# Four graph layers on one core: rows with exchanged batches, loads spread over the first stage, and the last group's third weight recorded into the second stage

## The chip, the cores and the metric

The kernel runs on one core of one Trainium2 chip. Its time is the device time of one execution in microseconds, and the time of a version is the median of its runs. One more execution was recorded by the hardware profiler; every row of a profile below comes from such an execution.

## The reference

`x` has 128 batches of 64 nodes and 256 features, `adj` is 64 x 64, and everything is float32. Four layers follow one another, each as a residual with a layer norm behind it. Cut to what matters:

```python
mix = lambda M, y: einsum('nm,bmh->bnh', M, y)
ln = lambda y: (y - mean(y)) / sqrt(var(y) + 1e-5)        # over the features

# layer 0: three graph steps 256 -> 512 -> 1024 -> 256
S = adj * adj
h = relu(mix(S, x @ W1)); h = relu(mix(S, h @ W2))
x = ln(x + mix(S, h @ W3))

# layer 1: spectral step with the eigenvectors U of adj's normalized Laplacian
h = relu(mix(U.T, x) @ W1 + b1)                            # 256 -> 128
x = ln(x + mix(U, h @ W2 + b2))                            # 128 -> 256

# layer 2: two graph steps, then an LSTM over windows of 1, 2, 3 and 4 nodes
h = relu(mix(adj, x @ Wg0 + bg0)); h = relu(mix(adj, h @ Wg1 + bg1))
for p in 1, 2, 3, 4:       # the last hidden state of each window replaces its last node
    h[last node of each window of p] = lstm_p(windows of h)
x = ln(x + h)

# layer 3: h = x @ W + b_lin; a = softmax over m of (h h^T * adj, zeros masked)
x = ln(x + a @ h + b)
```

## The kernel before

The 8192 rows form 64 row tiles of 128 rows, two batches to a tile, and four tiles (eight batches) form a group: 16 groups. A mixing step multiplies from the left by a 128x128 matrix that holds the 64x64 matrix twice on its diagonal (`adT2`, `sqT2` with the squares, `u2` and `ut2` for the eigenvectors).

**First stage** (`layer0`, called at L1228; groups in the order 4 to 15, then 0 to 3). The rows of the last four groups stay in SBUF (`X`, `RING = 4`). Those of the other twelve lie in `XA` until the stage is done, and each group's result goes to DRAM (`rest`), from where the second stage fetches it. The instruction order of PE, DVE, ACT and POOL is the order of the program text here (`manual_schedule`). For each group:

- `burst` (L1062) mixes and transposes a half of the rows at once: 32 products of 64x64 blocks (two instructions each in float32), four of them on different quarters of PE's array. Its tensors are `ps`, `sqT`, `X` or `h` in the trace.
- `seven` runs a 2x2 block product with seven instead of eight block products, for the first, second and third weight (`by_first`, `by_second`, `by_third`; L977 is the helper `mm` that all of them call). The additions that this needs are on DVE (`VL`, recorded at L52) and as adding DMAs (`adds`). A `step()` puts the copies or additions of one product behind the next one and emits one small step of a pending layer norm.
- the last group uses `plain` (L1121) for the third weight: four products of 8 x two 128x256 instructions, with no additions.
- `mix_rows` (L1136) mixes the result `s3` with `sqT2`: two float32 products of 128x512 in a group, one for each pair of row tiles. Their result is added to the rows, normed, and stored to `rest`.

The eigenvectors come from a Jacobi-like solver (`eigen`) whose steps are inserted between the products by a running clock (`now`, `between`); `u2` and `ut2` are ready at the end of the stage.

All loads are issued by SP ahead of the loop, in the order of the text: `adj`, the first group's rows, the first two weights, then the rows of all other groups with the third weight (`aw3`) after the second group (L921 to L924), then the constants of the solver and the weights and biases of the later layers (L943 to L959). Some small preparations stand behind the first stage in the text (L1235 to L1244: row sums of `adj`, biases added or halved); no manual order covers them, and a scheduler places their instructions.

**Second stage** (`Plan`). Layers 1 to 3 are recorded as operations with costs, and a list scheduler orders them on each engine before anything is emitted; all of them are emitted at L162. Work comes in units of two groups (`unit`), up to four in flight (`UNITS = 4`). Tiles of an operation come from counted slots, and an operation starts when its inputs and slots are there by the planned clock. The first recorded unit, `left_over`, holds the layer norm steps that the first stage has not yet emitted, and the later units depend on them by rows. The weights of the LSTMs (`wih`, `whh`, L1258 to L1267) get the same seven-product treatment, with their sums prepared in `add_weights` (L1305). The last unit (groups 14 and 15, `ENDING`) runs a different end: `from_lstm` (L1526) copies the hidden states `hT` from node-major to batch-major (`hb`), turns them on PE, adds and norms them; `layer3` (L1549) works in two halves and its last norm uses ACT for the scaling. `norm` (L1426) takes the statistics on DVE, and its `rs` (and, in that scalar form, `nm`) on POOL.

Of the kernel before, what the change touches and what calls it, by code (L numbers as in the profile page):

```python
# [16 lines left out]
N = 64  # L17
# [744 lines left out]
P = 128  # L762
# [15 lines left out]
RING = 4  # L778
QUADS = 1.17
# [61 lines left out]
def kernel(  # L841
# [28 lines left out]
    x_t = x.rearrange("b n f -> (b n) f").rearrange("(t p) f -> p t f", p=P)  # L870
    out_t = out.rearrange("b n f -> (b n) f").rearrange("(t p) f -> p t f", p=P)
# [32 lines left out]
    def given(g):  # L904
        return x_t[:, 4 * g:4 * g + 4, :]

    adst = keep.tile([P, N], F32, name="adst")
# [3 lines left out]
    nc.scalar.dma_start(rows_of(order[0])[:, 2:4, :], given(order[0])[:, 2:4, :])  # L911
    for t in range(2):
        nc.sync.dma_start(rows_of(order[0])[:, t, :], given(order[0])[:, t, :])
# [5 lines left out]
    for g in order[1:]:  # L919
        for t in (0, 2):  # L920
            nc.sync.dma_start(rows_of(g)[:, t:t + 2, :], given(g)[:, t:t + 2, :])  # L921
        if g == order[1]:
            aw3 = load(wa, "aw3", a_w3, "(k p) f -> p k f", [P, 8, D], p=P)
    nc.sync.dma_start(eig_c, consts)  # L924
# [11 lines left out]
    sqT2 = ea.tile([P, P], F32, name="sqT2")  # L936
# [14 lines left out]
    nc.sync.dma_start(cb1, c_b1)  # L951
    wide = {}
    for name, src in (("b_b1", b_b1), ("b_b2", b_b2), ("c_b0", c_b0), ("d_b", d_b)):
        wide[name] = keep.tile([P, src.shape[0]], F32, name=f"wide_{name}")
        nc.sync.dma_start(wide[name], src.partition_broadcast(P))
    cbi = keep.tile([P, 4, 8], F32, name="cbi")
    cbh = keep.tile([P, 4, 8], F32, name="cbh")
    nc.sync.dma_start(cbi, c_bi)
    nc.sync.dma_start(cbh, c_bh)  # L959
# [48 lines left out]
    h2 = pa.tile([P, 2, 8, 256], F32, name="h2")  # L1008
    sh = pa.tile([P, 4, 4, 256], F32, name="sh")
    s3 = pa.tile([P, 4, D], F32, name="s3")  # L1010
# [51 lines left out]
    def burst(dst, src, c):  # L1062
        to = dst.rearrange("p c (t h n) -> p h c t n", h=2, n=N)
        p = [bank().rearrange("p (c t n) -> p c t n", c=2, t=4) for _ in range(2)]
        for t in range(4):
            for k in range(2):
                for m, f, h, hs in quads(c + k):
                    PE.matmul(p[h][m, k, t, :], src[hs, t, f], sqT2[hs, hs], start=True, stop=True)  # L1068
        now[0] += QUADS
        between()  # L1070

        def result():
            for h in range(2):
                S.copy(to[:, h, c:c + 2], p[h])

        step(result)
# [44 lines left out]
    def plain():  # L1121
        for t in (0, 2):
            p = bank().rearrange("p (t f) -> p t f", t=2)
            for i in range(2):
                run(p[:, i, :], [(h2[:, t // 2, c, i * P:(i + 1) * P], aw3[:, c, :]) for c in range(8)])
                step((lambda p=p, t=t: S.copy(s3[:, t:t + 2, :], p)) if i else None)
                yield
        for _ in range(3):
            yield

# [5 lines left out]
    def mix_rows(g, t):  # L1136
        p = bank().rearrange("p (t f) -> p t f", t=2)
        mm(p, sqT2, s3[:, t:t + 2, :])

        def result():  # L1140
            x2 = rows_of(order[g])[:, t:t + 2, :]
            VL.tensor_add(x2, p, x2)
            norms.extend(scalar_norm(tc, small, x2, half, spare))
            if t and order[g] >= RING:
                norms.append(lambda: nc.sync.dma_start(rest[order[g]], rows_of(order[g])))

        step(result)

    def sums_second():
        S1, S2, S4 = (ss[:, i] for i in range(3))  # L1150
        VL.tensor_add(S1, A21, A22)
        VL.tensor_sub(S2, S1, A11)
        VL.tensor_sub(A21, A11, A21)
        VL.tensor_sub(S4, A12, S2)

    def layer0():
# [12 lines left out]
        for g in range(n):  # L1169
            last = g == n - 1  # L1170
            then = {} if last else {
                (1, 1): lambda: less(2, 0, 0),
                (1, 6): lambda: sums_first() if g else burst(m1, rows_of(order[1]), 0),
                (0, 5): lambda: (less(2, 1, 0), nc.sync.dma_start(sh[:, 1], sh[:, 2])),
                (0, 3): lambda: (nc.sync.dma_start(sh[:, 0], H22), adds(sh[:, 1], H22)),
                (0, 4): lambda: (less(3, 0, 1), None if g else sums_first()),
                (1, 3): lambda: [adds(sh[:, slot], H21) for slot in range(3)],
            }
            sums_second()
            w2 = [seven(256, by_second(j), *[h2[:, r, 4 * c + 2 * j:4 * c + 2 * j + 2, :] for r in (0, 1) for c in (0, 1)],  # L1180
                        relu, order=(1, 2, 6, 5, 7, 4, 3) if j else (1, 2, 6, 5, 7, 3, 4)) for j in range(2)]
            sums = [] if g else [signed_sums(), sums_of_weights(first[0], W12)]
            for j in (0, 0, 1, 0, 1, 0, 1, 0, 1, 1, 0, 0, 1, 1):
                then.get((j, next(w2[j])), lambda: None)()
                for some in sums[j:]:
                    next(some, None)
            if last:
                for t in (0, 2):
                    mix_rows(g - 1, t)
                for _ in plain():  # L1190
                    pass
                for t in (0, 2):
                    mix_rows(g, t)
                break
            w3 = seven(P, by_third, *[s3[:, r:r + 2, c:c + P] for r in (0, 2) for c in (0, P)], S.copy,
                       order=(1, 2, 5, 6, 7, 3, 4))
            w1 = seven(256, by_first, *[h1[:, r:r + 2, c:c + 256] for r in (0, 2) for c in (0, 256)], relu)
            next(w3)
            less(3, 1, 1)
            if g:  # L1200
                mix_rows(g - 1, 0)
            next(w1)
            next(w3)
            next(w1)
            VL.tensor_sub(X12, X12, sx[:, 1])
            if g:
                mix_rows(g - 1, 2)
            next(w1)
            next(w1)
            adds(sh[:, 3], sh[:, 1])  # L1210
            for w in (w3, w1, w3, w1, w1, w3):
                next(w)
            burst(m2, h1, 2)
            next(w3)
            burst(m2, h1, 0)
            next(w3)
            if g + 2 < n:
                burst(m1, rows_of(order[g + 2]), 0)
# [3 lines left out]
    with tc.manual_schedule(engines={mybir.EngineType.PE, mybir.EngineType.DVE, mybir.EngineType.Activation,  # L1222
                                     mybir.EngineType.Pool}):
# [11 lines left out]
    pr = bank()  # L1235
    PE.matmul(pr[:, :P], ones, adT2, start=True, stop=True)
    V.tensor_copy(rs_row, pr[:, :P])
    V.tensor_scalar(adH2, adT2, 0.5, None, op0=ALU.mult)
    V.tensor_reduce(rs_col, adst, AX.X, ALU.add)
    V.tensor_scalar(wide["c_b0"], wide["c_b0"], rs_col, None, op0=ALU.mult)  # L1240
    V.tensor_add(cbi, cbi, cbh)
    V.tensor_add(dbb, dbb, dbl)
    for q in (slice(0, 4), slice(6, 8)):
        V.tensor_scalar(cbi[:, :, q], cbi[:, :, q], 0.5, None, op0=ALU.mult)  # L1244
# [12 lines left out]
    psb = ctx.enter_context(tc.tile_pool(name="psb", bufs=1, space=bass.MemoryType.PSUM, reuse_waits="tile"))  # L1257
    wih, whh = [], []  # L1258
    for i in range(4):
        if i:  # L1260
# [6 lines left out]
        whh.append(load(wb, f"whh{i}", c_hh[i], "(k p) f -> p k f", [P, 2, 1024], p=P) if i else None)  # L1267
# [37 lines left out]
    def add_weights(p, ready):  # L1305
        ways[p] = []
        names = "igo" if p == 1 else "ifgo"
        for k, w in enumerate((wih[p - 1], whh[p - 1])):
# [6 lines left out]
            s, w = plan.tile("sums", [P, 3, nq, P], s), plan.tile("sums", [P, 2, nq * 2 * P], w)  # L1315
            a11, a12, a21, a22 = whole = quarters(w)
# [109 lines left out]
    def norm(x, scalar, eps=EPS, twice=False):  # L1426
# [4 lines left out]
        if twice:  # L1431
# [4 lines left out]
        if scalar:  # L1436
            nm = plan.tile("nm", [P, 2])
            G.tensor_scalar(nm, mv[:, :, 0], -1.0, None, op0=ALU.mult)
            G.tensor_tensor(nm, nm, rs, ALU.mult)
# [86 lines left out]
    def from_lstm(xs, hT, g):  # L1526
        if g in ENDING:
            hb = as3(work(), 2)
            for bs in (slice(0, 4), slice(4, 8)):
                for k, copy, cost in ((0, V.tensor_copy, 0.33), (1, S.copy, 0.56)):  # L1530
                    copy(as3(hb[:, k, :], 8)[:, bs, :], hT[:, k, :, bs].rearrange("p n b -> p b n"), cost=cost)
# [17 lines left out]
    def layer3(xs, g, first, nt):  # L1549
# [89 lines left out]
        for t in range(0, nt, 2):  # L1639
# [8 lines left out]
            at = 4 * g + first + t  # L1648
            for j in range(2):
                Q.dma_start(out_t[:, at + j, :], x2[:, j, :])  # L1650
# [113 lines left out]
    def long(hTs, p):  # L1764
# [6 lines left out]
        def write(h, o, t):  # L1771
            for w in range(2):
                turn_out(seen(h, w, p - 1), o[:, w], t[:, w])

        c, hs = state("c", 8 * nw), None
        for t in range(p):
            x = [[seen(k, w, t) for w in range(2)] for k in range(2)]
            new = state("hs", 8 * nw) if t < p - 1 else None
            fast(p, 8 * nw, x, hs, c, new, write)
            if p == 4 and t == 2:  # L1780
                plan.late = plan.ops[-1]
            hs = new

    def unit(groups):
# [8 lines left out]
        for g in groups:  # L1793
            plan.group = g + 1
            x = plan.tile("rows", [P, 4, D])
            there.append(plan.tile("rest", [P, 4, D], rest[g]))
            if g < RING:
                x.tile.real, x.tile.slot, x.tile.unit = rows_of(g), g, plan.unit
                plan.slots["rows"][g] = 1e9
                for i, op in enumerate(reversed(plan.pieces)):  # L1800
                    if g == RING - 1 - i // 14:
                        half = np.arange(4 * D) // (2 * D) == i // 7 % 2
# [6 lines left out]
        for p in (3, 4):  # L1809
            long(hTs, p)  # L1810
# [12 lines left out]
    def left_over():  # L1823
# [6 lines left out]
        plan.pieces = plan.ops  # L1830
# [47 lines left out]
```

## Time and profile before

| | before |
|---|---|
| device time, median of 3 runs | 2268.37 us (2267.16 to 2269.09) |
| profiled execution | 2269.74 us, span 2267.9 us |
| mean granted TensorE clock | 0.995 |
| DMA packets, moved | 95243, 163.05 MB |

The span is the time from the first to the last recorded instruction; the 1.84 us beside it lie around the recorded part. Times in the rows are microseconds from the start of the span. PE is the matrix engine, PEld its weight load, DVE the vector engine, ACT the scalar engine, POOL GpSimd, and SP the queue that issues most DMAs. A timeline row has the start, the time from first start to last end, engine, line, operation, output and inputs, the shape, and the number of instructions; in brackets stands the idle time ahead of it and what ended that. A float32 product appears as two matmul instructions.

The page's costliest groups are `ps<-w,wih` (572.8 us of PE in 2944 instructions) and `ps<-w,sums` (476.6 us in 3104), both of the LSTMs, and the chain of work that ended last runs through `ps` at L162 for 59% and `ch` at L977 for 15% of the span. The first stage lasts to about 820 us, some 49 us for a group, and the second from there to the end.

### The profile page before, as it was taken

The page shows a single profiled execution, that of the slowest core. Times are in us where ns is not written, and L with a number is a line of the kernel's source. Part 1 is how long each engine was busy: PE and PEld are TensorE (multiplying, and loading weights), DVE is VectorE, ACT ScalarE, POOL GpSimd, SP SyncE. Part 2 cuts the span into 40 slices and gives each one's busy share as a digit, 9 for nine tenths or more (in the row PEclk, how much of TensorE's full clock was granted, in tenths as well). Part 3 has the DMA queues.
Part 4 walks back from the last instruction along what each step waited for, and adds up shares of the span by engine and source line. Part 5 has one row for each costly group of instructions (what it writes and reads, how often), then busy time and mean ns, then how long its engine had stood idle before and what let it go on. Part 6 is the DMA issues. An engine that isn't in the chain of part 4 may idle for free.

```text
span 2267.9 us, 53164 instructions
## 1 busy us (share of the span) xinstructions
PE 2222.0 (98%) x20840; PEld 2026.8 (89%) x20840; DVE 1758.5 (78%) x5925; ACT 1241.2 (55%) x2999; POOL 207.9 (9%) x390
## 2 busy tenths in 40 slices
PE   7999999999999999999999999999999999999996
PEld 5998888888888878999999999999999999999985
DVE  5888888878888759765967977977977877578977
ACT  3455555545554445665655655655655655566554
POOL 0111111111111110000100000000000010000112
PEclk9999999999999999999999999999999999999998
DMA  8443333344332240000211211211211211002331
GB/s 264 96 92 77 85 75 85 87 91 94 85 85 66 66 155 29 20 1 20 76 38 41 78 66 50 78 57 50 87 57 41 84 65 35 31 29 65 109 113 54
DMA packets 95243, 163.05 MB, mean 72 GB/s; under 512 B 24976, under 2 KB 65936, under 8 KB 94992
## 3 DMA queue, kind: packets, MB, share of 16 engines
q1 hardware_dynamic: 83840, 120.05, 15.8%
q0 software_dynamic: 10800, 39.33, 9.2%
q8 instruction: 164, 2.69, 0.5%
q14 instruction: 87, 0.71, 0.1%
q10 hardware_dynamic: 352, 0.28, 0.0%
HBM read 57.64 MB, written 45.09 MB: 45 GB/s over the span
## 4 chain that ended last, share of the span: by engine, by line
PE 89%; DVE 6%; DMA 2%; ACT 1%; issue 1%; SPq 1%; POOL 1%; ACTq 0%; POOLq 0%; DVEq 0%
PE ps L162 59%; PE ch L977 15%; PE b L977 7%; PE ps L977 6%; PE ps L1068 2%; DVE w L162 1%; PE pa L312 1%; DVE D L52 1%; DMA XA<-in_x_dram 1%; DVE gates L162 1%; DVE X L162 1%; ACT gates L162 0%; DVE h L52 0%; DVE tw L52 0%; SPq L921 0%
## 5 line engine op out<-in xcount | busy, mean ns | idle before, releaser
L162 PE MATMUL ps<-w,wih 128*128 128x128 f32 (+2 forms) x2944 | 572.8, 298 | 2.1 <-DVE gates L162 0.9
L162 PEld LDWEIGHTS ps<-w,wih 128*128 128x128 f32 x2944 | 453.8, 191 | 28.5 <-issue 6.2
L162 PE MATMUL ps<-w,sums 128*128 128x128 f32 (+2 forms) x3104 | 476.6, 293 | 0.0
L162 PEld LDWEIGHTS ps<-w,sums 128*128 128x128 f32 x3104 | 423.5, 191 | 14.1 <-issue 1.9
L162 ACT ACTIVATE gates<-gates,cbi 128x256 f32<-128x256 f32 (+4 forms) x736 | 314.0, 479 | 174.0 <-DVE gates L162 172.0
L162 DVE TENSOR_TENSOR gates<-gates,ps 128x512 f32<-128x512 f32 (+4 forms) x408 | 234.2, 585 | 173.1 <-PE ps L162 159.7
L162 ACT COPY gates<-ps 128x512 f32<-128x512 f32 (+4 forms) x408 | 203.8, 505 | 253.8 <-PE ps L162 247.8
L986 ACT ACTIVATE h<-h 128x512 f32<-128x512 f32 x141 | 88.8, 629 | 283.3 <-DVE h L52 283.2
L162 PE MATMUL ps<-hs,whh 128*128 128x128 f32 (+1 forms) x896 | 181.2, 284 | 0.1
L162 PE MATMUL ps<-w,whh 128*128 128x128 f32 (+1 forms) x896 | 181.1, 284 | 0.0
L162 POOL TENSOR_SCALAR rs<-mv 128x2 f32<-128x2 f32 x96 | 27.5, 297 | 1318.5 <-DVE mv L162 1317.0
L162 ACT ACTIVATE gates<-ps,cbi 128x128 f32<-128x128 f32 (+2 forms) x368 | 119.1, 383 | 43.4 <-PE ps L162 43.1
L162 PEld LDWEIGHTS ps<-hs,whh 128*128 128x128 f32 x896 | 139.7, 191 | 0.3 <-DVE hs L162 0.3
L162 PEld LDWEIGHTS ps<-w,whh 128*128 128x128 f32 x896 | 139.7, 191 | 0.0
L977 PE MATMUL ch<-m,tw 128*128 128x256 f32 x512 | 120.6, 380 | 3.5 <-DVE h L52 3.5
L977 PE MATMUL b<-ss,aw 128*128 128x256 f32 x512 | 122.6, 379 | 0.0
L977 PEld LDWEIGHTS ch<-m,tw 128*128 128x128 f32 x512 | 96.2, 190 | 17.2 <-DVE h L52 4.7
L977 PEld LDWEIGHTS b<-ss,aw 128*128 128x128 f32 x512 | 96.3, 190 | 12.7
L1060 POOL DMA_DIRECT2D sh<-h x60 | 53.2, 957 | 485.9 <-PE b L977 148.8
L162 ACT ACTIVATE gates<-c 128x256 f32<-128x256 f32 (+1 forms) x176 | 75.5, 433 | 27.9 <-DVE c L162 26.2
L162 PE MATMUL ps<-hs,sums 128*128 128x128 f32 (+1 forms) x448 | 90.6, 284 | 0.0
L162 DVE TENSOR_TENSOR w<-w,w 128x128 f32<-128x128 f32 (+2 forms) x264 | 80.5, 316 | 8.9 <-PE ps L162 4.4
(384 smaller groups left out, 4281.2 us busy)
## 6 DMA issues: line engine op xcount, KB each, us to landing
sh<-h POOLq DMA_DIRECT2D x60, 512.0 KB, 5.8
far<-w SPq DMA_DIRECT2D x42, 512.0 KB, 2.8
w<-far SPq DMA_DIRECT2D x168, 128.0 KB, 3.1
X<-rest SPq DMA_DIRECT2D x24, 512.0 KB, 3.4
out_dram<-X SPq DMA_DIRECT2D x64, 128.0 KB, 1.8
sh<-sh SPq DMA_DIRECT2D x15, 512.0 KB, 2.9
sh<-h SPq DMA_DIRECT2D x15, 512.0 KB, 2.9
sh<-sh POOLq DMA_DIRECT2D x15, 512.0 KB, 4.6
```

Of the source, the lines that this page charges most:

```text
L52: return getattr(self.engine, name)(out, *args, **kw)
L162: getattr(e, name)(*[real(x) for x in args], **{k: real(v) for k, v in kw.items()})
L312: PE.matmul(out, lhsT, rhs, start=True, stop=True)
L977: PE.matmul(out, lhsT, rhs, start=start, stop=stop, **kw)
L986: S.activation(dst, src, AF.Relu)
L1060: nc.gpsimd.dma_start(out, src, accum_op=ALU.add)
L1068: PE.matmul(p[h][m, k, t, :], src[hs, t, f], sqT2[hs, hs], start=True, stop=True)
```

## The change

- **Rows with exchanged batches.** Before, half `h` of row tile `t` in a group holds batch `2t + h` of that group. After, tile `2u + j` holds batch `2h + j` of four in half `h` (`given`, `found`). `fetch` therefore loads two tiles by two DMAs of 64 partitions, and the output is stored the same way.
- **Row mixing in quarters.** `mix_rows` takes a whole group at once: eight products of 64x256 on quarters of the array, into two banks, in place of two of 128x512. The result is added and normed by halves `h` (tiles `h` and `h + 2`).
- **Loads spread.** Only the first four groups' rows (`AHEAD = 4`) are loaded ahead; group `g + 4` is fetched at the top of group `g`, with two of the loads in the list `later` (constants, weights, biases) beside it. SP is put into the first stage's manual order.
- **Small preparations** (`small_things`) run inside the first stage, at the end of the products with the second weight of group `n - 4`.
- **Third weight of the last group.** `plain` and its mix leave `layer0` and are recorded in `left_over`, so that the list scheduler places them. `aw3`, `h2`, `s3` and `sqT2` now live through both stages; `aw3` and `h2` share the tile `twice`, into which three LSTM weights (`c_ih[3]`, `c_hh[2]`, `c_hh[3]`) are loaded once those products are over (`plan.over`).
- **Norm.** In the scalar form, `rs` (the addition of epsilon) and `nm` (one instruction in place of two) are on DVE in place of POOL.
- **Ending.** The copies of `hT` to batch-major are made before the last LSTM step of `p = 4`, and that step writes its states there (`turned`).

```diff
+    given, found = (v.rearrange("(q h j) n f -> q h n j f", h=2, j=2) for v in (x, out))
+    def fetch(queue, g, u):
+        for h, hs in enumerate(halves):
+            queue.dma_start(rows_of(g)[hs, 2 * u:2 * u + 2, :], given[2 * g + u, h])
+    twice = keep.tile([P, 3, 8, D], F32, name="twice")
+    aw3, h2 = twice[:, 0], twice[:, 1:3]
...
-    for g in order[1:]:
-        for t in (0, 2):
-            nc.sync.dma_start(rows_of(g)[:, t:t + 2, :], given(g)[:, t:t + 2, :])
+    for g in order[1:AHEAD]:
+        for u in range(2):
+            fetch(nc.sync, g, u)
...
-    nc.sync.dma_start(eig_c, consts)
+    later = [(eig_c, consts)]
...
-    def plain():
-        for t in (0, 2):
-            p = bank().rearrange("p (t f) -> p t f", t=2)
-            for i in range(2):
-                run(p[:, i, :], [(h2[:, t // 2, c, i * P:(i + 1) * P], aw3[:, c, :]) for c in range(8)])
-                step((lambda p=p, t=t: S.copy(s3[:, t:t + 2, :], p)) if i else None)
...
-    def mix_rows(g, t):
-        p = bank().rearrange("p (t f) -> p t f", t=2)
-        mm(p, sqT2, s3[:, t:t + 2, :])
+    def mix_rows(g):
+        p = [bank().rearrange("p (u f) -> p u f", u=2) for _ in range(2)]
+        for u in range(2):
+            for j, js in enumerate(halves):
+                for h, hs in enumerate(halves):
+                    PE.matmul(p[h][js, u, :], sqT2[hs, hs], s3[hs, 2 * u + j, :], start=True, stop=True)
 
         def result():
-            x2 = rows_of(order[g])[:, t:t + 2, :]
-            VL.tensor_add(x2, p, x2)
-            norms.extend(scalar_norm(tc, small, x2, half, spare))
-            if t and order[g] >= RING:
-                norms.append(lambda: nc.sync.dma_start(rest[order[g]], rows_of(order[g])))
+            rows = rows_of(order[g])
+            for h in range(2):
+                VL.tensor_add(rows[:, h::2, :], p[h], rows[:, h::2, :])
+                norms.extend(scalar_norm(tc, small, rows[:, h::2, :], half, spare))
+            if order[g] >= RING:
+                norms.append(lambda: nc.sync.dma_start(rest[order[g]], rows))
...
+    def small_things():
...
         for g in range(n):
+            if g + AHEAD < n:
+                for u in range(2):
+                    fetch(nc.sync, order[g + AHEAD], u)
+            for to, of in later[2 * g:2 * g + 2]:
+                nc.sync.dma_start(to, of)
...
+            if g == n - 4:
+                small_things()
             if last:
-                for t in (0, 2):
-                    mix_rows(g - 1, t)
-                for _ in plain():
-                    pass
-                for t in (0, 2):
-                    mix_rows(g, t)
+                mix_rows(g - 1)
                 break
...
             if g:
-                mix_rows(g - 1, 0)
+                mix_rows(g - 1)
...
-            if g:
-                mix_rows(g - 1, 2)
...
+    wih[3], whh[2], whh[3] = late = [twice[:, i].rearrange("p (k a) f -> p k (a f)", k=2) for i in range(3)]
...
+            if any(w.tile.real is x for x in late):
+                Q.dma_start(w, (c_hh if k else c_ih)[p - 1].rearrange("(k p) f -> p k f", p=P), cost=0.35, after=plan.over)
...
-        if twice:
+        if scalar:
+            V.tensor_scalar(rs, mv[:, :, 1], eps, None, op0=ALU.add)
+        elif twice:
...
-            G.tensor_scalar(nm, mv[:, :, 0], -1.0, None, op0=ALU.mult)
-            G.tensor_tensor(nm, nm, rs, ALU.mult)
+            V.scalar_tensor_tensor(nm, mv[:, :, 0], -1.0, rs, op0=ALU.mult, op1=ALU.mult)
...
     def from_lstm(xs, hT, g):
         if g in ENDING:
-            hb = as3(work(), 2)
-            for bs in (slice(0, 4), slice(4, 8)):
-                for k, copy, cost in ((0, V.tensor_copy, 0.33), (1, S.copy, 0.56)):
-                    copy(as3(hb[:, k, :], 8)[:, bs, :], hT[:, k, :, bs].rearrange("p n b -> p b n"), cost=cost)
+            hb = hT.rearrange("p k b n -> p k (b n)")
...
+            if ending and new is None:
+                for hT in hTs:
+                    turned.append(work().rearrange("p (k b n) -> p k b n", k=2, b=8))
+                    for k, copy in ((0, V.tensor_copy), (1, S.copy)):
+                        copy(turned[-1][:, k], hT[:, k].rearrange("p n b -> p b n"), cost=0.8 if k else 0.6)
             fast(p, 8 * nw, x, hs, c, new, write)
...
     def left_over():
...
+        s, x = plan.tile("s3", [P, 4, D], s3), plan.tile("rows", [P, 4, D], rows_of(order[-1]))
+        for t in (0, 2):
+            p = ps4((P, 2, D))
+            for i in range(2):
+                for c in range(0, 8, 2):
+                    plan.note("PE", [("matmul", (p[:, i, :], h2[:, t // 2, k, i * P:(i + 1) * P], aw3[:, k, :]),
+                                      {"start": k == 0, "stop": k == 7}) for k in (c, c + 1)], 0.87,
+                              after=plan.ops[-1] if i + c else None)
+            plan.over = plan.ops[-1]
+            S.copy(s[:, t:t + 2, :], p)
+        q = [ps4((P, 2, D)) for _ in range(2)]
+        plan.note("PE", [("matmul", (q[h][js, u, :], sqT2[hs, hs], s[hs, 2 * u + j, :]), {"start": True, "stop": True})
+                         for u in range(2) for j, js in enumerate(halves) for h, hs in enumerate(halves)], QUADS)
+        for h in range(2):
+            V.tensor_add(x[:, h::2, :], q[h], x[:, h::2, :])
+            norm(x[:, h::2, :], True)
+        plan.last = x
```

## The prediction

> **What bounds the kernel now.** I read the page's busy shares and its chain first, then PE's waits, a table of stretches, and PE's and DVE's timelines where PE is not full.
>
> ```profile
> PE 2222.0 (98%) x20840; PEld 2026.8 (89%) x20840; DVE 1758.5 (78%) x5925; ACT 1241.2 (55%) x2999; POOL 207.9 (9%) x390
> PE 89%; DVE 6%; DMA 2%; ACT 1%; issue 1%; SPq 1%; POOL 1%; ACTq 0%; POOLq 0%; DVEq 0%
> ```
>
> PE is the bound: a microsecond of product taken away counts wherever PE is full, and idle PE is in three places. The first is the start, where DVE stands behind two loads and PE behind DVE:
>
> ```profile
> 44.48 0.16 DVE L1242 TENSOR_TENSOR dbb<-dbb,dbl 128x2 f32<-128x2 f32 x1 [5.17 <-DMA dbb<-in_d_b_dram]
> 48.24 0.35 DVE L1240 TENSOR_SCALAR wide_c_b<-wide_c_b,rs_col 128x256 f32<-128x256 f32 x1 [2.70 <-DMA wide_c_b<-in_c_b_dram]
> ...
> 45.69 0.46 PE L312 MATMUL pa<-AQ,LV 128*128 128x128 f32 x2 [2.07 <-DVE LV L52]
> 49.24 1.99 PE L977 MATMUL ch<-m,tw 128*128 128x256 f32 x8 [0.51 <-DVE h L52]
> 53.68 1.99 PE L977 MATMUL ch<-m,tw 128*128 128x256 f32 x8 [2.44 <-DVE h L52]
> ```
>
> The second is the seam of the stages: 17.65 us of PE alone (804.02 to 821.67) while DVE has little, then some 60 us in which DVE is full and PE is not. Columns: stretch, its length, busy PE, PEld, DVE, ACT, POOL, granted clock, DMA share, GB/s.
>
> ```profile
> 800.00:825.00 25.00, 24.50 (x226) 19.95 (x225) 4.96 (x9) 8.63 (x24) 2.00 (x5) 1.00 0.39 133
> 825.00:850.00 25.00, 21.24 (x473) 18.44 (x475) 22.55 (x59) 14.05 (x40) 7.78 (x17) 0.93 0.55 214
> 850.00:875.00 25.00, 22.01 (x229) 18.34 (x219) 23.60 (x54) 14.47 (x28) 1.77 (x4) 0.99 0.08 25
> ...
> 805.74 13.98 PE L977 MATMUL ps<-aw,h 128*128 128x256 f32 x64
> 837.63 3.43 PE L162 MATMUL ps<-bw,v 128*128 128x256 f32 x8 [2.70 <-DVE v L162]
> ```
>
> The third is the end, a chain of small steps after the last LSTM product (2224 to 2265). Between, from 60 to 804 and from 885 to 2170, PE idles under 4 us.
>
> **The change, part by part.** *Start.* The additions at L1239 to L1244 leave the head of DVE's queue and run in group `n - 4` of the first stage (`small_things`), and their loads no longer stand behind twelve groups of rows. The PE waits 2.07 + 0.51 + 2.44 = 5.0 us go. What is late next: the second `h<-h,ch` sum follows 3.3 us of eigen steps that need the product now at 43.6, so it ends near 47.6, and PE wants it at 48.1: nothing new. A stall of 1.60 us at 27.05 that the profile puts down to issue, while the DMA share is 1.1, may go too: 0 to 1.6, I take 0. Start: -5.0.
>
> The loads are the same bytes as 64-partition copies, twice as many issues: 0.43 us each, four in each of twelve groups and two small ones in the first eight, at most 2.6 us of SP ahead of the `sh` copies. SP issues nothing between 600.64 and 628.82 in a steady group and the rows are four groups (some 195 us) early: nothing. Without that cover it would be up to 2.6 us for each of twelve groups.
>
> *Row mixing.* Two 128x512 products become eight of 64x256 on quarters of the array. The rows that bear on it:
>
> ```profile
> 607.68 1.02 PE L977 MATMUL ps<-s,sqT 128*128 128x512 f32 x2
> 608.54 1.03 PE L977 MATMUL ch<-aw,m 128*128 128x256 f32 x4
> ...
> 627.10 2.05 PE L977 MATMUL ch<-tv,h 128*128 128x128 f32 x16
> 629.08 1.16 PE L1068 MATMUL ps<-sqT,X 64*64 64x64 f32 x64
> 630.17 1.99 PE L977 MATMUL ch<-m,aw 128*128 128x256 f32 x8
> 632.00 1.89 PE L977 MATMUL ps<-m,aw 128*128 128x256 f32 x8
> ```
>
> From start to start, a 128x512 mix takes 0.86 us, two 1.72. A 256-column instruction takes 1.73 / 8 = 0.216 us. The burst passes 64 instructions of 64 columns in 1.09 us, 17 ns each where one after the other would need 54 ns: better than three run at once. So 16 instructions of 256 columns need 16 x 0.216 / 4 = 0.86 us at best, 1.09 at the burst's overlap of 3.2. Around a burst there is a toll: the sixteen products ahead take 1.98 us (627.10 to 629.08) against 1.79 elsewhere, the eight behind 1.83 against 1.73: 0.29 in all. 0.93 + 0.29 = 1.22 us, nearer the streaming end since long instructions hide issue; 0.50 saved in each of 15 groups: -7.5. Ends: -12.9 (no toll, four at once) and +4.5 (only two at once: 1.73 + 0.29 is 0.30 more, 15 times). The Trainium skill, TensorEngine Tiling, Tiling Modes, says that a change of tiling mode drains the array while tiles of one mode run in parallel. That speaks against more switches; the 0.29 us agrees, and without such a drain the sum would have 12.9 here instead of 7.5.
>
> The mix now takes two banks of three at once and its sums stand together on DVE, which is 88% busy there (43.9 of 50 us): the next product on that ring is over 2 us later, the sums take 1.3. Nothing; up to 0.5 us a group if not.
>
> *Seam.* The 64 instructions of the third weight (13.9 us) and the last mix are recorded in the second stage's plan; the order built from the changed kernel puts 26 of their 32 products among the products ahead of the first `hs,whh`, and six and the mix behind it. Before, that first `hs,whh` stands at 884.60, 62.9 us after 821.67. By the rows' times PE's products in it are 49.1 us, so 13.8 us is idle (8.2 in the waits listed), slow clock or switching. After, they are 57.8 us and DVE's work falls from 53.7 to 51.1 us, since group 3's come later. With both engines nearly full I take 63.5 us for the stretch (62 to 68). Saved: 17.65, less 1.22 for the mix that stays, 2.6 + 1.2 for what is left to do after it, 2.6 for group 3's products passed on, 0.6 longer stretch: -9.4, from -11 to -5. The weights that share SBUF with `h2` and `aw3` come after the last of these products, about 100 us ahead of their first use. What is late next: the eigenvectors. `u2` stood 34 us ahead of its first use (787.7 to 821.67); now nine products and a mix cover it, 5.1 us. It fits, barely.
>
> Part of it is clock: the products at 837.63, behind 2.70 us of idle PE, took 3.43 us where eight take 1.73, at a granted clock of 0.72 from 835 to 840. That 1.7 us is within the 13.8. The Trainium skill, TensorE: Matmul & The Clock Gate, Part 1, has the clock halved only after an idle window of about 3.4 us; by that this loss would stay outside the change, and the sum 1.7 us smaller. The trace has it after 2.70 us, and decides.
>
> *End.* The copies of `hT` (2226.84 to 2228.1 on the path) go ahead of the last cell: -1.2. `nm` leaves POOL, two steps of about 0.2 us and a hand-over, for one on DVE, at three places of the path: -0.4 each, -1.2. The addition of `eps` moves from POOL to DVE too, one hand-over later: -0.2 each, -0.6. But the built order ends with both last norms together: four sums and four activations where there were two, +1.1. That is -1.9, taken as -2.0. An order built anew may move a wait of the size of the 2.42 us at 2176.90 either way: from -5 to +3.
>
> **Sum.** -5.0 - 7.5 - 9.4 - 2.0 = -23.9 us. The profiled execution took 2269.74 (span 2267.9 and 1.84 around it), 1.4 over the median of 2268.37, inside the runs' 1.9; taken from the median: 2244.5.
>
> **Rivals.** *DVE and the eigen chain pace the first stage.* The DVE column (88% from 560 to 760) speaks for it, PE's full 50 of 50 us against. Eigen ended at 790.25, 782.4 without the 7.87 us of DVE waits; shorter groups then only make PE wait at its steps. The 7.5 is lost: 2252. *The seam hides nothing:* DVE is the bound there, each inserted product delays the one that DVE wants, and only 2 of 9.4 remain: 2252 as well. *The quarters do not overlap at 256 columns*, since they stream different data, where the burst's share one operand: 16 x 0.216 + 0.29 = 3.75 us, +2.03 x 16 = +32.5 in place of -8.0 for the 16 mixes, which turns the sum to +16.6: 2285, slower. It decides from 2.7 us for a mix on; the burst's 17 ns speaks against it. *The order does not change what is late:* waits of the start and seam come back elsewhere, 2268.
>
> **How the numbers follow.** Forecast 0.62, eigen chain 0.17, seam 0.13, no overlap 0.05, no change 0.03. About 0.2% (4.5 us) is what can be told from no change. Faster 0.92, same 0.03, slower 0.05. The range reaches from all better ends at once (6.6 + 12.9 + 11 + 5 = 35.5 less, 2233) to both losing rivals at once (2252 and the seam's 7.4 more, 2260); no overlap alone lies outside.
>
> **What would show it.** DVE without the two waits on loads before 60 us; 15 mixes of 1.2 us; products of `twice` between 800 and 870 with DVE busy from the start and PE's idle under 3 us; the first `hs,whh` near 856; the end some 40 us after the last LSTM product. Wrong, if PE waits on `u` or `UT` at the seam, or mixes over 1.7 us.

## The result, and the profile after

The changed kernel takes 2252.44 us (median of 6 runs, 2250.95 to 2253.19) beside 2269.06 us for the kernel before (2267.16 to 2271.35 in the same runs): ratio 0.9923, 95% interval 0.9911 to 0.9934, so 16.6 us less where 23.9 were forecast. The profiled execution has a span of 2251.0 us, 16.9 less than before. The page's busy shares and its chain, as shown of before:

```profile
PE 2214.4 (98%) x21032; PEld 2024.7 (90%) x21032; DVE 1758.7 (78%) x5951; ACT 1237.9 (55%) x2981; POOL 197.8 (9%) x362
PE 89%; DVE 6%; ACT 2%; DMA 1%; issue 1%; SPq 0%; POOL 0%; ACTq 0%; DVEq 0%; POOLq 0%
```

PE is still the bound, with 7.6 us less of busy time; the other 9.3 us of the span are idle PE that is gone. The start on PE's timeline, with the same eigen product (`pa`) and the same products with `tw` as before:

```profile
44.14 1.03 PE L986 MATMUL ch<-m,tw 128*128 128x256 f32 x4
45.00 0.38 PE L312 MATMUL pa<-AQ,LV 128*128 128x128 f32 x2
45.22 1.03 PE L986 MATMUL ch<-m,tw 128*128 128x256 f32 x4
...
47.81 3.62 PE L986 MATMUL ch<-m,tw 128*128 128x256 f32 x16
```

There is no wait in brackets any more: the 2.07, 0.51 and 2.44 us are gone. A steady group, with the mixing as quarter products:

```profile
499.07 1.95 PE L986 MATMUL ch<-twice 128*128 128x128 f32 x16
500.95 1.09 PE L1140 MATMUL ps<-s,sqT 64*64 64x256 f32 x16
501.97 1.13 PE L986 MATMUL ch<-aw,m 128*128 128x256 f32 x4
502.94 0.61 PE L986 MATMUL ps<-twice 128*128 128x128 f32 x4
```

From start to start the mix takes 1.02 us. The sixteen products ahead take 1.88 (1.79 elsewhere) and the four behind 0.97 (0.86), so its toll is 0.20 and a mix costs 1.22 us, the figure that was forecast. The seam, first PE and then the stretches of before:

```profile
796.98 1.09 PE L1140 MATMUL ps<-s,sqT 64*64 64x256 f32 x16
798.87 2.09 PE L162 MATMUL ps<-u,X 64*64 64x64 f32 x128 [0.80 <-DVE X L52]
...
806.14 1.99 PE L162 MATMUL ps<-twice 128*128 128x256 f32 x8
...
859.72 0.39 PE L162 MATMUL ps<-hs,whh 128*128 128x128 f32 x2
```

```profile
800.00:825.00 25.00, 24.47 (x404) 21.27 (x395) 21.69 (x57) 11.12 (x31) 6.83 (x14) 1.00 0.52 190
825.00:850.00 25.00, 24.65 (x290) 21.04 (x290) 21.76 (x49) 12.25 (x21) 1.73 (x4) 1.00 0.10 35
850.00:875.00 25.00, 24.84 (x190) 23.28 (x189) 17.81 (x51) 15.12 (x36) 0.00 (x0) 1.00 0.06 22
```

Products with `twice` (the third weight of the last group) now stand among the second stage's, DVE is busy from 800 on where it had 4.96 us of 25 before, and PE's clock is 1.00 throughout (0.93 and 0.99 in the second and third stretch before).

Five places on PE's timeline divide the whole. In the last column stands what the prediction's terms give for each stretch; 0.5 us of its sum (the fifteenth mix, in both the mixing and the seam) was counted twice and is in no row.

| stretch | before | after | difference | forecast |
|---|---|---|---|---|
| start to the burst of the third group's rows | 79.12 | 76.16 | -2.96 | -5.0 |
| from there to the burst of the last group's rows | 647.25 | 642.37 | -4.88 | -6.5 |
| to the end of the last seven products | 77.65 | 78.45 | +0.80 | -0.5 |
| to the first `hs,whh` | 80.58 | 62.74 | -17.84 | -15.8 |
| to the end | 1383.30 | 1391.28 | +7.98 | +4.4 |

From the fourth burst on, a group's length in the first stage repeats between kernels within some 0.02 us wherever its instructions are the same (49.14 or 49.15 us from the sixth to the seventh burst in every kernel that has the quarter products), so places on this timeline resolve differences that the medians can't. Ahead of it they don't: from the third to the fourth burst the same instructions take 50.13 to 50.43 us. In the text below, group 12 is the one with the small preparations; its length is from the burst at 620.31 to that at 670.73.

### The profile page after: what moved, and what is told of

Its sections match the earlier page's. It is cut to its first block, busy times and chain, and to the rows that moved or that the text cites. A ratio compares the mean times of both kernels' runs of the same rounds, so it can differ in the third digit from the quotient of the medians.

```text
span 2251.0 us, 53589 instructions
## 1 busy us (share of the span) xinstructions
PE 2214.4 (98%) x21032; PEld 2024.7 (90%) x21032; DVE 1758.7 (78%) x5951; ACT 1237.9 (55%) x2981; POOL 197.8 (9%) x362
## 3 DMA queue, kind: packets, MB, share of 16 engines
q1 hardware_dynamic: 84320, 120.05, 16.6%
HBM read 57.64 MB, written 45.09 MB: 46 GB/s over the span
## 4 chain that ended last, share of the span: by engine, by line
PE 89%; DVE 6%; ACT 2%; DMA 1%; issue 1%; SPq 0%; POOL 0%; ACTq 0%; DVEq 0%; POOLq 0%
PE ps L162 60%; PE ch L986 15%; PE b L986 7%; PE ps L986 4%; PE ps L1077 2%; ACT gates L162 1%; PE pa L312 1%; DVE D L52 1%; DMA sh<-twice 1%; DVE tw L52 1%; PE ps L1140 1%; DVE w L162 1%; DVE gates L162 0%; DVE X L162 0%; DVE st L162 0%
## 5 line engine op out<-in xcount | busy, mean ns | idle before, releaser
L162 PE MATMUL ps<-w,wih 128*128 128x128 f32 (+2 forms) x1984 | 400.7, 309 | 1.0 <-DVE w L162 0.5
L162 PEld LDWEIGHTS ps<-w,wih 128*128 128x128 f32 x1984 | 309.2, 191 | 21.3 <-issue 4.9
L162 PE MATMUL ps<-w,twice 128*128 128x128 f32 (+1 forms) x1600 | 255.0, 281 | 0.0
L162 PEld LDWEIGHTS ps<-w,twice 128*128 128x128 f32 x1600 | 219.8, 191 | 6.4 <-issue 1.6
L995 ACT ACTIVATE twice<-twice 128x512 f32<-128x512 f32 x96 | 60.4, 630 | 219.7 <-DVE twice L52 219.6
L162 PE MATMUL ps<-hs,twice 128*128 128x128 f32 (+1 forms) x640 | 132.0, 288 | 1.3 <-DVE hs L162 1.0
L162 POOL TENSOR_SCALAR rs<-mv 128x2 f32<-128x2 f32 x88 | 21.8, 258 | 1166.5 <-DVE mv L162 1165.7
L162 PEld LDWEIGHTS ps<-hs,twice 128*128 128x128 f32 x640 | 100.8, 191 | 1.9 <-DVE hs L162 1.4
L1067 POOL DMA_DIRECT2D sh<-twice x60 | 53.1, 956 | 497.4 <-ACT twice L995 214.5
L162 POOL TENSOR_TENSOR rs<-rs,half 128x2 f32<-128x2 f32 x98 | 73.9, 768 | 174.2 <-DVE rs L162 155.0
```

The costliest lines, as they stand in the source:

```text
L162: getattr(e, name)(*[real(x) for x in args], **{k: real(v) for k, v in kw.items()})
L995: S.activation(dst, src, AF.Relu)
L1067: nc.gpsimd.dma_start(out, src, accum_op=ALU.add)
```

## Experiments

Each of these is the changed kernel with the edit shown, cut to what matters; those behind "Versions beyond the change" combine several. Times are medians, and ratios are to the kernel before.

**The mixing as two products of 128x512, rows in the old order.**

```diff
-    given, found = (v.rearrange("(q h j) n f -> q h n j f", h=2, j=2) for v in (x, out))
+    given, found = (v.rearrange("(q j h) n f -> q h n j f", h=2, j=2) for v in (x, out))
...
-            for j, js in enumerate(halves):
-                for h, hs in enumerate(halves):
-                    PE.matmul(p[h][js, u, :], sqT2[hs, hs], s3[hs, 2 * u + j, :], start=True, stop=True)
+            mm(p[u], sqT2, s3[:, 2 * u:2 * u + 2, :])
...
```

> The changed kernel with the rows in the old order (half h of tile t holds batch 2t + h) and each group's mixing as two products of 128x512 again, both at the place of the eight quarter products; loads, small preparations, seam and end stay as changed. Theory 1, PE paces the first stage and the quarters save 0.5 us a group: fifteen mixes in the stage and one behind it give back about 8 us, so 2260 us, with the end of the last seven products moving from 796.98 to about 804.5. Rival, DVE and the eigen steps pace the stage: 2252 to 2254 us and that end at 797 to 799.

2262.12 us (0.9966, 0.9952 to 0.9979), 9.7 more than the changed kernel, and the last seven products end at 806.89. From the third burst to the last the stage takes 652.29 us, 9.92 more: 0.76 for each of 13 groups. What a mix takes longer is passed on in full, so PE paces this part of the stage, and the rival by which DVE and the eigen steps do falls. The 0.76 is more than the prediction's 0.50, and the kernel before needs 647.25 us for the same stretch. PE's listed waits in it come to 4.1 us here, 2.5 in the changed kernel and 1.8 before, so waits explain a part of it. The two products stood at two places before; here both stand at one and hold two banks, which is probably the reason; it was not tried by itself.

**The last group's third weight back in the first stage.**

```diff
+                plain()
+                mix_rows(g)
                 break
...
-            x = plan.last if g == order[-1] else plan.tile("rows", [P, 4, D])
+            x = plan.tile("rows", [P, 4, D])
...
```

> The changed kernel with the last group's third weight and mixing back at the end of the first stage, not recorded in the second. Theory 1, the products fill idle PE at the seam: between the end of the last seven products and the last LSTM product 9.3 us were saved, all of it comes back, 2262 us, and the first product of hs with an LSTM weight stands again 80 us behind the last seven products (62.7 in the changed kernel). Rival, the seam hid only 2 us and the rest was saved by other rows of the second stage's new order: 2254 to 2256 us.

2261.77 us (0.9969, 0.9957 to 0.9981), 9.3 more. The first `hs,whh` stands at 877.38, 81.56 us behind the last seven products (795.82), and from it to the end are 1382.52 us, 8.76 fewer than in the changed kernel. So the move saves 18.8 us ahead of that product, gives 8.8 back behind it, and the time shows about the rest. That is the forecast's 9.4 beside the new ending; beside the old one it is another figure, as the runs of the end show.

**The small preparations: three ways to take their cost away.** First the order on DVE alone:

```diff
-        V.tensor_copy(rs_row, pr[:, :P])
+        step(lambda: V.tensor_copy(rs_row, pr[:, :P]))
```

> The changed kernel, but in the small preparations the copy of the row sums (rs_row) on DVE is put behind the next product instead of directly behind its own. Theory 1, DVE's wait of 2.05 us for that product is what makes group 12 last 50.4 us where its neighbours last 47.8: about 2 us less, 2250.5, with that group at 48.5 us. Rival, the 1.6 us of added DVE work in a group where DVE is 87% busy is the cost: group 12 stays above 50 us and the time within 0.5 us of 2252.4.

2252.37 us (0.9924, 0.9912 to 0.9937). Group 12 lasts 49.84 us, 0.58 less than the 50.42, and 2 more than its neighbours' 47.80. Both theories missed the group, the rival by 0.2 us (it has the time right). The wait that the edit was to take away, on DVE in the changed kernel, is this:

```profile
646.10 0.29 DVE L1164 COPY rs_row<-ps 128x128 f32<-128x128 f32 x1 [2.05 <-PE ps L1163]
```

With the edit DVE waits 1.83 us at 646.81 instead, for the product (`b`) ahead of it: `step` also brings forward the sum that was pending. So this run doesn't show what the wait is worth. Then the place:

```diff
-            if g == n - 4:
-                small_things()
             if last:
+                small_things()
                 mix_rows(g - 1)
```

> The changed kernel with the small preparations at the end of the last group's products in place of group 12's. Theory 1, they cost 2.5 us only where DVE is full of eigen steps: group 12 goes back to 47.9 us and, as DVE is half idle from 770 to 795, the last seven products end near 794.5 and the time is about 2250. Rival, the eigen chain is late by the same amount at the stage's end wherever they stand: PE waits for u or for X at the seam and the time stays at 2252 to 2253.

2251.75 us (0.9919, 0.9906 to 0.9933). Group 12 lasts 47.80 us, so the preparations cost 2.62 us there. Half of it comes back: the last seven products end 78.93 us behind the last burst (78.45 in the changed kernel), and the second stage's first product follows 2.68 us behind the start of the last mix, not 1.89. What is left is 1.35 us. Each theory is right on one side, by the trace; the medians (2251.75 and 2252.44) differ by less than their intervals. Third, the engine:

```diff
-        V.tensor_copy(rs_row, pr[:, :P])
-        V.tensor_scalar(adH2, adT2, 0.5, None, op0=ALU.mult)
-        V.tensor_reduce(rs_col, adst, AX.X, ALU.add)
+        step(lambda: S.copy(rs_row, pr[:, :P]))
+        S.activation(spare[0]()[:, :N], adst, AF.Identity, accum_out=rs_col)
+        nc.gpsimd.tensor_scalar(adH2, adT2, 0.5, None, op0=ALU.mult)
...
```

> The changed kernel with the small preparations of group 12 taken off DVE: the copy of the row sums and the sum of adst on ACT, the other six on POOL. Theory 1, the 2.6 us that they cost are DVE's 1.6 us and its order in a group where DVE is 87% busy: group 12 lasts 47.8 to 48.1 us as its neighbours do, nothing comes back at the seam (the last group has no work of theirs), the last seven products end 2.3 to 2.6 us earlier than in the changed kernel for the same start, and the time is about 2250. Rival, it is the additional product and the bank that it takes on PE that cost: group 12 stays above 49.5 us and the time at 2252.

2251.16 us (0.9922, 0.9908 to 0.9936). Group 12 lasts 49.13 us, between the two expectations: half of the 2.62 goes, half stays. On PE's timeline of the changed kernel and then of this one the same product with `aw,m` waits behind the mix:

```profile
645.68 0.38 PE L1163 MATMUL ps<-adT,ones 128*128 128x128 f32 x2
...
653.17 1.13 PE L986 MATMUL ps<-aw,m 128*128 128x256 f32 x4 [1.06 <-DVE XA L52]
```

```profile
644.10 0.38 PE L1164 MATMUL ps<-adT,ones 128*128 128x128 f32 x2
...
650.29 1.13 PE L986 MATMUL ps<-aw,m 128*128 128x256 f32 x4 [0.15 <-DVE XA L52]
...
655.36 1.13 PE L986 MATMUL ch<-tu,m 128*128 128x256 f32 x4 [0.22 <-ACT h L1125]
```

With the preparations off DVE the wait for the sums of the mix (`XA`) falls from 1.06 to 0.15 us; what stays is the product itself (0.22 from start to start), two waits of 0.37 together and slower products around them (1.06 and 0.97 from start to start, where four take 0.86). The wait for `XA` is for a sum that frees a bank: the mix holds two of the three banks, and the added product takes a turn in the same ring. But DVE isn't out of it, since the `step` of this edit brings the pending sum forward here too:

```profile
644.30 0.69 DVE L52 TENSOR_TENSOR twice<-twice,b 128x512 f32<-128x512 f32 x1 [1.83 <-PE b L986]
...
649.54 1.29 DVE L52 TENSOR_TENSOR XA<-ps,XA 128x512 f32<-128x512 f32 x2
```

The sums of the mix start 3.34 us behind the mix (646.20) in this kernel, 4.64 in the changed one, and 1.65 in the kernel below whose group 12 has nothing of the preparations. How much of the half that stays is DVE's wait, and how much the product and its bank, was not separated.

**All loads ahead again.**

```diff
-    for g in order[1:AHEAD]:
+    for g in order[1:]:
...
-            if g + AHEAD < n:
-                for u in range(2):
-                    fetch(nc.sync, order[g + AHEAD], u)
-            for to, of in later[2 * g:2 * g + 2]:
-                nc.sync.dma_start(to, of)
...
+    for to, of in later:
+        nc.sync.dma_start(to, of)
```

> The changed kernel with all loads issued ahead of the first group again (rows of all groups, then the list later), still as copies of 64 partitions; the small preparations stay in group 12. Theory 1, the start gained because DVE no longer stands behind the small loads' sums, not because loads are spread: from the burst of the second group's rows to that of the third stays 36.7 us (41.2 before), and the time is 2252 to 2254 us. Rival, the traffic itself (DMA share 1.1 to 45 us) delays the copies that the third weight's products read: that stretch goes back toward 41 us and the time to 2256 to 2257.

2268.88 us (1.0000, 0.9990 to 1.0009): the whole gain is gone. Neither theory has the reason. On SP's queue and on PE:

```profile
8.29 33.85 SPq L907 DMA_DIRECT2D XA<-in_x_dram  x40
42.19 11.31 SPq L907 DMA_DIRECT2D X<-in_x_dram  x16
...
62.59 0.55 SPq L1191 DMA_DIRECT2D sh<-sh  x1
63.24 0.54 SPq L1192 DMA_DIRECT2D sh<-twice  x1
```

```profile
74.40 1.62 PE L986 MATMUL b<-tv,sh 128*128 128x128 f32 x6 [15.49 <-DMA sh<-twice]
```

The first copy of `sh` stands behind 56 issues of rows and 15 of small loads and leaves at 62.59, where the kernel before issued it at 45.09 and the changed kernel at 39.28. PE then waits 15.49 us. In the changed kernel the second copy is issued at 49.45, and the same product has this row:

```profile
60.80 0.91 PE L986 MATMUL b<-tv,sh 128*128 128x128 f32 x6 [0.39 <-DMA sh<-twice]
```

From that issue to the product it is 11.16 us here (63.24 to 74.40) and 11.35 there. So the copies and the additions behind them aren't slower for the traffic (a DMA share of 0.68 from 40 to 60, 0.56 in the changed kernel); they are issued later. The first theory's own step did hold, since PE has no wait between 38 and 58 although the small loads are issued from 53.54 on: DVE doesn't stand behind them. So the two parts of the start do different work. Moving the preparations removes the 5.0 us; by SP's rows, spreading the loads pays for the row order, whose copies of half the size are twice as many (56 issues in 45.2 us, where the kernel before has 28 in 26.9).

**The first group's rows by one tile to a copy, on two queues.**

```diff
-    fetch(nc.scalar, order[0], 1)
-    fetch(nc.sync, order[0], 0)
+    for t in range(4):
+        for queue, h, hs in zip((nc.sync, nc.scalar), range(2), halves):
+            queue.dma_start(rows_of(order[0])[hs, t, :], given[2 * order[0] + t // 2, h][:, t % 2, :])
```

> The changed kernel with the first group's rows loaded as eight copies of 64 partitions and one tile, halves on two queues (SP and ACT), so that a tile is complete earlier than with two tiles to a copy. Theory 1, the first burst waits 3.0 us for rows because a tile now needs two copies that each hold two tiles: the burst of the second group's rows moves from 39.5 (38.0 to 40.3 in the kernels with the same loads) to about 38.0, and the time is 2251. Rival, its place varies by the landing of the loads and by the clock of the start alone, not by their form: it stays at 38 to 40.3 and the time at 2252.4.

2251.64 us (0.9920, 0.9906 to 0.9935); the burst of the second group's rows stands at 38.27. The ten kernels with the changed kernel's form of these loads have it from 37.54 to 40.82 (the changed kernel 39.49), so one profile can't tell the form from the scatter of the start. The run is inconclusive; the two later kernels with this edit have it at 37.11 and 37.08, below all ten, which speaks for the first theory with about 1 us.

**The end: the copies of `hT`, the norm on POOL, and both.**

```diff
+            hb = as3(work(), 2)
...
-            long(hTs, p, p == 4 and groups[0] in ENDING)
+            long(hTs, p, False)
```

> The changed kernel with the copies of hT to batch-major back behind the last LSTM step. The prediction's term: the copies were 1.2 us of the path, so the stretch from the last LSTM product to the end goes from 43.3 to 44.5 us. Rival, their time is now taken by four DVE steps of another group's attention (X<-ps,sm,X, 0.47 us each) that the planner put between the cell's steps, and would otherwise stand behind the copies: 43.3 within 0.6 us, and the time within 1 us of 2252.4.

```diff
-        if scalar:
-            V.tensor_scalar(rs, mv[:, :, 1], eps, None, op0=ALU.add)
-        elif twice:
+        if twice:
...
-            V.scalar_tensor_tensor(nm, mv[:, :, 0], -1.0, rs, op0=ALU.mult, op1=ALU.mult)
+            G.tensor_scalar(nm, mv[:, :, 0], -1.0, None, op0=ALU.mult)
+            G.tensor_tensor(nm, nm, rs, ALU.mult)
```

> The changed kernel with rs and nm of the scalar norm on POOL again. The prediction's term: 0.6 us at each of three norms on the path, so the stretch from the last LSTM product to the end goes from 43.3 to 45.1 us and the time to 2254. By the two traces the wait from the second addition to the first transposition behind it is 0.87 us longer on POOL (4.59 against 3.72), which would give up to 2.6 us. Rival, the planner orders the end anew and hides it behind other groups' products: 43.3 within 0.6.

> The changed kernel with both changes of the end undone: the copies of hT behind the last step, rs and nm on POOL. Alone they cost 1.3 and 2.3 us in the stretch from the first product of hs with an LSTM weight to the end (1391.3 us in the changed kernel, within 0.5 over the kernels with the same end). Theory 1, they are separate steps of one chain and add: 1394.9 us, and the time is 2256. Rival, the planner's order of the end is what counts: before and the kernel with the seam undone differ there by only 0.8 us (1383.3 and 1382.5), so both undone cost about 0.8: 1392.1 us, and the time is 2253.

(Without its branch, `rs` of the scalar norm falls to the `else` of that text, on POOL.) In the first two the planner moves products behind the last LSTM product (46.66 and 47.73 us are left behind it, 43.31 in the changed kernel, and it comes 2.1 us earlier behind the first `hs,whh`), so the stretch from the first `hs,whh` to the end is the one to compare: 1391.28 in the changed kernel (1390.51 to 1391.55 in the eight others with the same end), 1392.55 without the early copies, 1393.61 with the norm on POOL, 1397.83 with both. Times: 2253.56 (0.9930, 0.9915 to 0.9945), 2254.19 (0.9933, 0.9916 to 0.9949) and 2257.93 (0.9947, 0.9931 to 0.9964). Alone they are worth 1.3 and 2.3 us in this stretch, which is near the prediction's 1.2 and 1.8, though the first is little more than the scatter; by the times, the intervals of both overlap with the changed kernel's. Together they are worth 6.5, not 3.6, and beside the old seam less than 1: before and the kernel with the old seam differ by 0.78 in this stretch. The same holds the other way round. With the old ending, the new seam saves 17.5 us ahead of the first `hs,whh` (80.58 before, 63.06 with both undone) and gives 14.5 back behind it (1383.30 and 1397.83), so it is worth 3.0 us there and 10.1 beside the new ending, both by the traces. The terms don't add. Every edit of the recorded operations gives a new planned order, which is the likely reason.

**Versions beyond the change.** The preparations on ACT and POOL with the first group's loads as above:

> The same with the first group's rows as eight copies on two queues. Both changes stand in different stretches, so their savings add: if the small preparations save 2.4 us and the loads 0.8 (2252.44 to 2251.64 in the run with the loads alone), 2249.2 us; by the rival, under which the loads' run only had an earlier start by chance, no less than the kernel without them, about 2250.

2250.68 us (0.9924, 0.9912 to 0.9936); the burst of the second group's rows stands at 37.11, group 12 at 49.14. The same in the last group:

> The changed kernel with the small preparations on ACT and POOL and in the last group instead of group 12, and the first group's rows as eight copies on two queues. Theory 1, no product stands behind the mix's two banks there and DVE has nothing of theirs at the seam: group 12 lasts 47.8 us, the last seven products end some 78.5 us behind the last burst as in the changed kernel, 2.6 us less for them, and the time is 2249 to 2250. Rival, the added product and ACT's copy delay the mix and the sum that the second stage starts with: 1.3 us of it come back there, as with the preparations on DVE in the last group, and the time stays at 2250.7.

2248.82 us (0.9910, 0.9895 to 0.9925), the lowest time here and 3.6 below the changed kernel, though the two intervals overlap. What the trace shows of it: group 12 lasts 47.80 us (2.62 less), the last seven products end 78.95 us behind the last burst (0.50 more), and the second stage's first product follows 1.89 us behind the last mix, as in the changed kernel. That is 2.1 us; in the one profile 2.9 more lie ahead of the third burst, where the scatter is as large.

## Why the prediction came out as it did

The direction and the range held, and the experiments bear out most of the mechanisms; the size fell short by 7.3 us (7.0 by the two profiled spans). By the table, the 7.0 are 2.0 at the start, 1.6 from the third burst to the last, 1.3 behind it, 1.5 over the two stretches from the seam to the end together, and the 0.5 that was counted twice. The time is also the 2252 that the prediction gave two of its rivals (DVE paces the first stage; the seam hides nothing), so the time alone would not tell them apart; the kernels with the mixing and with the seam undone, 9.7 and 9.3 us slower, speak against both.

- **Start, -5.0.** The three DVE waits went, as said. From the second to the third burst the kernel before takes 41.18 us and the changed one 36.67: -4.5. But the profiled execution reached the second burst 1.55 us later, within the scatter above, and two waits of 0.39 us on `sh` copies came in. The loads' issues cost PE nothing in the steady groups, as said. The term held in the stretch that has the waits, and single profiles of the start carry more than 1 us of chance.
- **Where the preparations went, priced at nothing.** This is the step that failed. The prediction asks what is late next where it takes the additions away, and gives the nine instructions of `small_things` no cost in group `n - 4`, where it has DVE at 88% itself. They cost 2.62 us there, the largest single piece of the shortfall; how that divides between DVE, the added product and its bank stays open. Without them the stretch from the third burst to the last would be 7.5 us shorter than before, or 0.58 a group.
- **Row mixing, -7.5.** 1.22 us for a mix, toll included, as forecast from the burst's rows; that the sum fits to the hundredth is luck, since its parts are each off by 0.09 (0.93 + 0.29, measured 1.02 + 0.20). The toll agrees with what the Trainium skill, TensorEngine Tiling, Tiling Modes, says of a drain at a change of mode. The rival without overlap (3.75 us) falls. That the mix holds two banks of three shows no wait for its sums except in group 12, where DVE was late and another product shared the ring (the 1.06 us above). Behind the last burst the term failed: the stretch is 0.80 us longer, where 0.5 less was due, and with the two products back it takes 77.29 us, 1.16 less than in the changed kernel. PE's listed waits in it are 2.0 us both before and after, and 1.1 with the two products back, so they explain a part of the 1.16 and not the 0.80; that cause stays open.
- **Seam, -9.4.** 9.3 us by the time of the kernel with it undone. That the two agree so well is in part luck: beside the old ending the seam is worth 3.0, and seam and end together come to 9.9 by the table, where 11.4 were forecast. PE fills what had been idle better than forecast: the first `hs,whh` is 62.74 us behind the last seven products, where the terms give 64.8 (80.6 less 15.8), and more is passed on behind it. The eigenvectors did fit: PE waits for `X` (0.80 us), not for `u`. Of the 1.7 us of half clock at 837 nothing is left, since PE no longer idles there (longest wait from 800 to 875: 0.34 us).
- **End, -2.0.** The single terms were nearly right (1.3 and 2.3 when undone), but the stretch from the last LSTM product to the end only went from 43.70 to 43.31 us. By DVE's rows the copies' time was taken by four `X<-ps,sm,X` steps that the planner put among the cell's last steps (not tried by itself), and both last norms come together as foreseen. What failed is that these terms were added to the seam's as if they were separate; the range of -5 to +3 for the new order covers it.

## What to carry to other kernels

A step that is moved off a stall has a price at its new place: look up which engine is full there, which ring of banks it enters, and who is queued behind it, before its old wait is counted as won. When copies are made smaller, count their issues on the queue that also carries the next stage's transfers: here the order of SP's queue, not the traffic, was worth 16 us. Work at a seam of two stages is best judged by undoing it, because part of what it saves ahead of a place is handed on behind it: 8.8 of 18.8 us here. Where a planner orders all of it anew, undo it beside each of the other edits too, since its worth depends on them: 3.0 or 10.1 us here.

## What was not expected of the hardware

Issues of row loads took SP 0.96 us each for copies of 256 KB (28 in 26.9 us before, by 21.38 + 5.54) and 0.81 for those of 128 KB (56 in 45.2 us, by 33.85 + 11.31, with all loads ahead): half the size cost SP nearly the same, so the same bytes took it 1.7 times as long. In the steady groups of the changed kernel four of them take 3.5 us, 0.88 each, twice the 0.43 that the prediction took from the small loads; an `sh` copy of 512 KB takes 0.52. It is hidden there. And behind a PE wait of as little as 0.15 us, the next groups of four 256-column products took 1.06 and 0.97 us from start to start where 0.86 is usual, so a short wait cost more than its own length here.
